# Reordering the step of two cross-attention layers: queries, keys and values, values product, fold, scores, then the whole output; plain keys and values in the first group

## The chip, the cores and the metric

The program runs on one core of one Trainium2 chip. The core has five engines that run side by side, each working through its own list of instructions in order: TensorE (PE in the profile; PEld is its weight load), VectorE (DVE), ScalarE (ACT), GpSimd (POOL) and SyncE (SP), whose list here only starts DMA transfers. The metric is the time of one execution on the device in microseconds (us); the number given for a kernel is the median of the runs shown.

## The reference, cut to what matters

Thirty-two sequences of 64 rows (2048 rows in all, width 512) go through two layers, each a cross-attention and a feed-forward part with residuals.

```python
x = x + xattn0(layernorm(x), ctx, ctx, mask1, wq, wk, wv, wo)   # 32 query heads, 8 key/value heads of 128
x = x + ffn0(layernorm(x), 4-bit weights, scales, zeros)        # silu(gate) * up, width 1376
x = x + xattn1(layernorm(x), ctx, mask0, ...)                   # same sizes; q and k rms-normed over the head
x = x + memory(layernorm(x), ...)                               # top-8 of 128 slots, gated
# xattn0:  q = rope(h @ wq);  k = rope(ctx @ wk);  v = ctx @ wv
#          w = softmax(where(mask, q @ k.T / sqrt(128), -1e9));  out = (w @ v) @ wo
```

`ctx` (32 x 64 x 512) is the same in both layers. Everything is float32.

## The kernel before, in words

**Steps.** Rows are handled in four chunks of 512 (`NCH` = 4, a chunk being eight sequences), heads in eight groups `g` of four query heads and one key/value head (`NKV` = 8). An attention layer is a loop of 32 steps `(g, c)` over groups and, inside, chunks (`Attention.run`, from L753). TensorE does, per step, six kinds of work; the names are those of the PSUM tiles in the profile:

- P: the queries of the next step, normed rows times `wq` (`project_q` L503, through `quarters` L222)
- KV: keys and values of the next step, context times `wkv` (`project_kv` L397)
- po: the values product of this step, probabilities times values (`values` L672)
- pm: layer 1 only, a fold of sums of squares for the rms norms (`norms` L546)
- S: the scores of the next step (`scores` L575)
- O: this step's output, `oT` times `wo`, added to the rows `x` (`out_product` L698, `join` L265)

**Seven products.** P, O and KV use a Strassen-like scheme: operands are cut 2 x 2 and seven block products take the place of eight. `PRODUCTS` (L181) names the left and right block of each product. Blocks 0 to 3 are the operand (two of them, blocks 1 and 2, are later overwritten), blocks 4 to 6 are sums, made on POOL by `left_sums` (L183) or `right_sums` (L194), four operations per operand. Products 1, 2 and 4 of O need none of the left sums; products 6, 5, 3 and 7 do. The products share PSUM tiles: 6 is added onto 1's tile after that has been copied out or added, 3 onto 5's, 7 onto 6's. There are six PSUM tiles `mm` for all of P, KV, po, pm and O, and one double tile `st` for S.

**The way from P and KV to S.** In layer 0, `quarters` copies each quarter of the queries out of PSUM on ACT (`h`, L237), adds on DVE (L514), makes a turned copy on ACT (`rq`, L494), multiplies by cosine and sine on DVE (L497, L498) and adds into `qT` on POOL (L499). The keys go the same way from `kx` through `rk` to `kT`. There are two tiles `tmp` for the turned copies. S needs all of `qT` and `kT`. In layer 1, instead of the rotation, squares are made and summed; pm folds the sums, `qs` is made on DVE and POOL raises it to the power -1/2 (`qr`, L277).

**The rest of a step.** `softmax` (L592) is a generator whose pieces run on DVE, ACT and POOL between the products of an output. `turn_v` (L474) transposes the values on DVE and writes them through 16 DMAs into the one tile `v`. The four po tiles are copied to `oT` on ACT (L693).

**The order in the text of a step.** For step `i` the kernel before writes: the last five products of the output of step `i-1` (`output_rest` L716: 4, 6, 5, 3, 7) with the softmax of step `i` between them; P of `i+1`; po of `i`; KV of `i+1`, with the copies of po and the first half of `left_sums(oT)` written into it (L431 to L434); the second half of `left_sums(oT)`; the first two products of the output of step `i` (`output_first` L708: 1, 2), in layer 1 with pm between; S of `i+1`.

**What sets the real order.** The lists of the engines are made when the program is built. The framework plays the program through with its own estimates of durations, and on each engine takes, of the instructions whose inputs and buffers are ready, the one that is written first. So an instruction written later can come ahead when an earlier one isn't ready in the estimate. `tc.issue_after(ins)` only adds that what is inside comes behind `ins` in its engine's list. On the chip the lists are fixed.

**Context and weights.** A chunk's context is two tiles `ctx` (two buffers, so one chunk at a time), loaded on SP after KV of the step before has read them (`load_ctx` L106). The first time a chunk is met, its four raw blocks are loaded, `ctx_sums` (L121) makes the sums on POOL (eight operations) and stores all seven blocks in `kept`; later loads take the seven blocks from there. In the kernel before that is group 0 of layer 0. `wq` and `wo` share two buffers, `wkv` has one. `att0.start` (L744) does KV and P of the first step.

**Buffers the change touches.** `half` (4) holds `kx`, `vx`, `vt` and the quarters `h`; `m2` (4) holds normed rows, spread columns of the softmax and the raw mask, chunk by chunk (`load_mask` L153, `mask_flags` L158); `sp` (1) holds the softmax's `s`.

Of the kernel before, what the change touches and what calls it, by code (L numbers as in the profile page):

```python
# [44 lines left out]
def tile_xattn_ffn_2_layers(ctx: ExitStack, tc: tile.TileContext, a: dict, out: bass.AP):  # L45
# [105 lines left out]
    mraw = {}  # L151

    def load_mask(c):  # L153
        w = NH * KH * S
        mraw[c] = m2_tile(f"mraw{c}")
        nc.sync.dma_start(mraw[c][:, 0:w], a["mask1"][:, c * w : (c + 1) * w])

    def mask_flags(c):  # L158
        w = NH * KH * S
        nc.vector.tensor_scalar(  # L160
            minv[:, c].rearrange("p f q -> p (f q)"), mraw[c][:, 0:w], 0.0, None, ALU.is_equal
        )
# [189 lines left out]
    class Attention:  # L352
# [44 lines left out]
        def project_kv(self, g, c, ctxT, copies=lambda js: None, sums=lambda: None):  # L397
# [4 lines left out]
            kx, vx = half_tile(f"kx{n}"), half_tile(f"vx{n}")  # L402

            def mul(which, ps=None):
                new = ps is None
                if new:
                    ps = mm_tile(f"KV{which}_{n}")
                l, r = PRODUCTS[which]
                for k in range(2):
                    nc.tensor.matmul(  # L410
                        ps[:, lo],
                        wkv[:, l, k, :],
                        ctxT[k][:, r, :],
                        start=(new and k == 0),
                        stop=(k == 1),
                        skip_group_check=True,
                    )
                return ps

            def copy(dst, cols, ps):  # L420
                return nc.scalar.copy(dst[:, cols], ps[:, lo]).ins
# [4 lines left out]
            copies((0, 1, 2))  # L426
            x = mul(1)
            with tc.issue_after(copy(kx, lo, x)):
                copies((3,))
            sums()  # L430
            y = mul(2)  # L431
            w = mul(5)
            copy(vx, hi, w)
            add(kx, lo, y)  # L434
            mul(6, x)
            copy(kx, hi, x)
            mul(3, w)
            add(kx, hi, w)
            k, rest = self.finish_k(n, kx)
            mul(7, x)  # L440
            copy(vx, lo, x)
            add(vx, hi, x)
            self.keyed = rest()
            add(vx, lo, mul(4))
# [29 lines left out]
        def turn_v(self, g, c, vx):  # L474

            n = f"{self.L}_{g}_{c}"
            vt = half_tile(f"vt{n}")
# [194 lines left out]
        def values(self, g, c, v, probs):  # L672
# [18 lines left out]
            def copies(js):  # L691
                for j in js:
                    ins = nc.scalar.copy(o5[:, j], po[j].rearrange("p (x q) -> p x q", q=S))  # L693
                self.copied = ins.ins

            return oT, copies
# [11 lines left out]
        def output_first(self, g, c, oT, middle=lambda: None):  # L708
# [3 lines left out]
            middle()  # L712
            self.out_add(c, 0, 0, self.out_product(g, c, oT, 2))
            return g, c, oT, x

        def output_rest(self, g, c, oT, x, pieces=None, middle=lambda: None):  # L716

            at = (0, 1, 2, 4) if self.L == 0 else (0, 2, 2, 4)  # L720
            result = []

            def behind(k):
                if pieces is not None:
                    for _ in range(at.count(k)):
                        result[:] = [next(pieces)]

            behind(0)
            z = self.out_product(g, c, oT, 4)
            behind(1)  # L730
            self.out_add(c, 1, 0, z)
            self.out_product(g, c, oT, 6, x)
            self.out_add(c, 0, 1, x)
            behind(2)
            middle()
            self.out_add(c, None, 1, self.out_product(g, c, oT, 5), 1)
            behind(3)
            self.out_add(c, 0, 1, self.out_product(g, c, oT, 3))
            behind(4)
            self.out_product(g, c, oT, 7, x)  # L740
            self.out_add(c, 1, None, x, 2)
            return result[0] if result else None

        def start(self):  # L744
            left_sums(self.wkv[0], HD)
            ctx_sums(0, self.ctx)
# [6 lines left out]
        def run(self, hooks, joined, after, between=lambda c: None, tail=lambda: None, late={},  # L753
# [8 lines left out]

            def ctx_of(i):
                return load_ctx(steps[i][1], f"{self.L}_{steps[i][0]}_{steps[i][1]}")

# [6 lines left out]
            for i, (g, c) in enumerate(steps):  # L772
                more = i + 1 < len(steps)
                if c == NCH - 1 and g + 1 < NKV:
                    self.load_kv(g + 1)
# [807 lines left out]
```

## Time and profile before

| | us |
|---|---|
| median of 3 runs | 2889.42 |
| lowest and highest | 2886.56, 2892.95 |
| the profiled execution | 2894.53 |
| its span, first to last instruction | 2892.7 |
| layer 0's attention, from the third values product to the 31st | 158.09 to 1185.24 |
| layer 1's attention, from the second to the 30th | 1743.45 to 2692.06 |

The span is 1.8 us shorter than the profiled execution's time; what lies around it is not in the profile. Busy shares are averages over stages. The digits of the profile's second part are tenths of a slice of 72.3 us. A timeline row has start, duration, engine, line, operation, tiles and count; in square brackets is the idle time of the engine before it and what ended that. TensorE's matmuls are pipelined and their ends modelled, so the distance between the starts of two groups is a better measure of a group's length than its own duration, which overlaps the next.

### The profile page before, as it was taken

What the parts mean: (1) busy time and instruction counts of PE and PEld (TensorE: products, weight loads), DVE (VectorE), ACT (ScalarE), POOL (GpSimd) and SP (SyncE); (2) the same over time, 40 slices, a digit from 0 to 9 for tenths busy, and PEclk for the clock granted to TensorE, in tenths of its full rate; (3) what the DMA queues carried; (4) which work ended last, traced back from release to release, by engine and by line L of the source; (5) the groups of instructions that cost most, each with busy time, mean ns of one, the idle gap of its engine ahead of it and who ended that gap; (6) DMA issues with size and microseconds to landing.
All of it is one profiled execution on the core that took longest, in us unless ns stands there. A gap on an engine that the chain in (4) does not pass through costs nothing.

```text
span 2892.7 us, 42394 instructions
## 1 busy us (share of the span) xinstructions
PE 2783.6 (96%) x15974; PEld 2272.0 (79%) x15974; DVE 2031.9 (70%) x3109; ACT 886.4 (31%) x1609; POOL 1391.9 (48%) x1147
## 2 busy tenths in 40 slices
PE   5999999999999999999999989999999999999998
PEld 4787777777877787788888778888888888888775
DVE  6778888877787777855665666666666666666667
ACT  2433333333333333321111232222222222222244
POOL 6654545454545454553333445454545454545332
PEclk8999999999999999999999999999999999999999
DMA  5232222222222222200000112222222222222111
GB/s 188 64 106 73 81 74 80 70 75 73 85 66 81 65 81 73 63 28 23 23 22 9 62 59 81 74 81 74 81 73 81 73 89 85 88 74 82 45 33 59
DMA packets 238098, 202.21 MB, mean 70 GB/s; under 512 B 157333, under 2 KB 213773, under 8 KB 237895
## 3 DMA queue, kind: packets, MB, share of 16 engines
q1 hardware_dynamic: 237319, 198.46, 21.7%
q8 instruction: 127, 2.08, 0.3%
q10 hardware_dynamic: 576, 1.05, 0.1%
q14 instruction: 76, 0.62, 0.1%
HBM read 171.11 MB, written 11.53 MB: 63 GB/s over the span
## 4 chain that ended last, share of the span: by engine, by line
PE 65%; DVE 15%; ACT 8%; POOL 5%; issue 5%; SPq 1%; DMA 1%; DVEq 0%; ACTq 0%; POOLq 0%
PE P L212 25%; PE O L212 18%; PE KV L410 9%; PE D L212 4%; PE S L583 4%; ACT rq L494 3%; PE po L684 2%; DVE x L272 2%; ACT oT L693 2%; POOL qT L499 1%; DVE rq L498 1%; DVE h L514 1%; SPq L483 1%; DVE h L497 1%; ACT rk L494 1%
## 5 line engine op out<-in xcount | busy, mean ns | idle before, releaser
L212 PE MATMUL O<-wo,oT 128*128 128x256 f32 x3584 | 820.0, 384 | 0.7 <-DVE x L272 0.5
L212 PE MATMUL P<-xnT,wq 128*128 128x256 f32 x3584 | 791.0, 380 | 10.1 <-ACT h L237 9.8
L212 PEld LDWEIGHTS O<-wo,oT 128*128 128x128 f32 x3584 | 672.6, 190 | 126.7 <-issue 23.9
L212 PEld LDWEIGHTS P<-xnT,wq 128*128 128x128 f32 x3584 | 680.8, 190 | 110.4 <-ACT h L237 15.6
L410 PE MATMUL KV<-ctx,wkv 128*128 128x256 f32 x1736 | 414.5, 390 | 30.8 <-ACT oT L693 23.2
L410 PEld LDWEIGHTS KV<-ctx,wkv 128*128 128x128 f32 x1736 | 321.6, 191 | 119.9 <-ACT oT L693 34.1
L664 POOL TENSOR_TENSOR s<-s,ib 128x512 f32<-128x512 f32 x128 | 168.6, 1339 | 475.5 <-DVE ib L343 465.6
L272 DVE TENSOR_TENSOR x<-x,O 128x512 f32<-128x512 f32 (+1 forms) x448 | 365.5, 816 | 44.5 <-PE O L212 44.2
L237 ACT COPY h<-P 128x512 f32<-128x512 f32 (+1 forms) x352 | 202.4, 575 | 633.9 <-PE P L212 609.9
L658 ACT ACTIVATE s<-s 128x1024 f32<-128x1024 f32 x64 | 67.7, 1057 | 803.4 <-DVE s L656 803.4
L499 POOL TENSOR_TENSOR qT<-h,rq 128x512 f32<-128x512 f32 x128 | 163.2, 1275 | 228.1 <-DVE rq L498 177.0
L212 PE MATMUL P<-xnT,wgu 128*128 128x256 f32 (+1 forms) x1232 | 271.4, 380 | 0.2
L212 PEld LDWEIGHTS P<-xnT,wgu 128*128 128x128 f32 (+1 forms) x1232 | 229.7, 187 | 40.2 <-DVE x L272 4.1
L497 DVE TENSOR_TENSOR h<-h,cosT 128x512 f32<-128x512 f32 x128 | 146.5, 1145 | 91.8 <-ACT rq L494 91.5
L187 POOL TENSOR_TENSOR oT<-oT 128x512 f32<-128x512 f32 x64 | 81.4, 1272 | 251.3 <-ACT oT L693 251.3
L494 ACT COPY rq<-h 64x512 f32<-64x512 f32 x256 | 157.9, 617 | 142.4 <-DVE h L514 115.3
L424 DVE TENSOR_TENSOR kx<-kx,KV 128x256 f32<-128x256 f32 x128 | 53.3, 417 | 171.8 <-PE KV L410 158.4
L1063 DVE TENSOR_TENSOR h<-h,P 128x512 f32<-128x512 f32 (+1 forms) x96 | 61.1, 640 | 128.6 <-PE P L212 92.9
L1070 POOL TENSOR_TENSOR hT<-h,h 128x512 f32<-128x512 f32 (+1 forms) x48 | 56.6, 1182 | 192.6 <-DVE h L1063 192.6
L693 ACT COPY oT<-po 128x512 f32<-128x512 f32 x256 | 139.9, 602 | 24.4 <-PE po L684 23.7
L583 PE MATMUL S<-qT,kT 128*32 128x256 f32 x2048 | 125.5, 386 | 16.6 <-POOL qT L499 9.5
L684 PE MATMUL po<-s,v 32*128 32x256 f32 x2048 | 131.8, 391 | 9.1 <-POOL s L664 8.4
(270 smaller groups left out, 3483.9 us busy)
## 6 DMA issues: line engine op xcount, KB each, us to landing
ctx<-kept SPq DMA_DIRECT2D x118, 896.0 KB
v<-vt SPq DMA_DIRECT2D x1024, 16.0 KB
wq<-in_L_wq SPq DMA_DIRECT2D x32, 256.0 KB
wo<-in_L_wo SPq DMA_DIRECT2D x32, 256.0 KB
wq<-in_L_wqT SPq DMA_DIRECT2D x32, 256.0 KB
wo<-in_L_woT SPq DMA_DIRECT2D x32, 256.0 KB
kept<-ctx SPq DMA_DIRECT2D x6, 896.0 KB
wgu<-in_qweight_gu SPq DMA_DIRECT2D x40, 128.0 KB
```

The source lines that it names most:

```text
L187: tt(b[4], b[2], b[3], ALU.add)
L212: ins = nc.tensor.matmul(pv[0:w, m, :], left[:, l, k, m * P : m * P + w], right[:, r, k, :], start=(first and m == 0 and k == 0), stop=(k ...
L237: last_copy = nc.scalar.copy(t[size], ps[size]).ins
L272: return nc.vector.tensor_tensor(dst, dst, src, ALU.add).ins
L410: nc.tensor.matmul(ps[:, lo], wkv[:, l, k, :], ctxT[k][:, r, :], start=(new and k == 0), stop=(k == 1), skip_group_check=True,)
L494: nc.scalar.copy(t[lo:hi], x[HD - hi : HD - lo])
L497: nc.vector.tensor_tensor(view(x), view(x), over(cosT), ALU.mult)
L499: return nc.gpsimd.tensor_tensor(dst(None), dst(x), dst(t), ALU.add).ins
L583: nc.tensor.matmul(s5[j * KB : (j + 1) * KB, f, e], kT[:, f, e, j], qT[:, f * 4 + j].rearrange("p h q -> p (h q)"), start=True, stop=True,)
L664: nc.gpsimd.tensor_tensor(sv[:, f], sv[:, f], ib[:, f * W : (f + 1) * W].unsqueeze(1).to_broadcast([P, KH, W]), ALU.mult,)
L684: nc.tensor.matmul(po[j][:, f * W : (f + 1) * W], v[rows, f, e], probs[rows, f, e], start=(e == 0), stop=(e == KH - 1),)
L693: ins = nc.scalar.copy(o5[:, j], po[j].rearrange("p (x q) -> p x q", q=S))
```

## The change

The diff does four things.

1. **Order of a step.** For step `i` the text is now: P of `i+1`, KV of `i+1` (in the very first step KV before P), po of `i`, the copies to `oT`, the values' transpose, pm, S of `i+1`, `left_sums(oT)`, and then all seven products of the output of step `i` (`output`: 1, 2, 4, 6, 5, 3, 7) with the softmax of step `i+1` between them. `output_first` and `output_rest` are gone, the sums of `oT` are written in one piece, and the copies of po are no longer written into KV. S keeps an `issue_after(last_matmul)`, which now is the last matmul of P.
2. **Plain keys and values in group 0 of layer 0.** There, eight block products take the place of seven, on the raw blocks (32 matmul records of 128x256 in place of 28); K is finished first and copied in one piece, then V. No sums of `wkv` or of the context are made for them.
3. **Sums of the context one group later.** `ctx_sums` runs in the steps before group 1's KV, so groups 0 and 1 load raw blocks, and `kept` is used from group 2 on.
4. **Buffers and loads.** `vx` and `vt` move from `half` to `m2`; the mask is loaded and turned into flags whole, in the `sp` tile, in place of by chunk; loads and sums of the next group's `wkv` and `wq` move from the last chunk's step to the one before it.

```diff
+    def load_mask():
+        mraw.append(sp_tile("mraw"))
+        nc.sync.dma_start(mraw[0].rearrange("p f w -> p (f w)"), a["mask1"])
+
+    def mask_flags():
...
@@ -394,54 +396,65 @@
-        def project_kv(self, g, c, ctxT, copies=lambda js: None, sums=lambda: None):
+        def project_kv(self, g, c, ctxT):
...
-            kx, vx = half_tile(f"kx{n}"), half_tile(f"vx{n}")
-
-            def mul(which, ps=None):
+            kx, vx = half_tile(f"kx{n}"), m2_tile(f"vx{n}")
+
+            def mul(l, r, ps, cols, first, last):
+                for k in range(2):
...
+            if self.L == 0 and g == 0:
+                for i, x in ((0, kx), (1, vx)):
+                    ps = mm_tile(f"pkv{i}_{n}")
+                    for f, cols in enumerate((lo, hi)):
+                        mul(2 * i, f, ps, cols, f == 0, False)
+                        mul(2 * i + 1, 2 + f, ps, cols, False, True)
+                    nc.scalar.copy(x, ps)
+                    if i == 0:
+                        k, rest = self.finish_k(n, kx)
+                rest()
+                return k, vx
+
+            def product_of(which, ps=None):
...
-            copies((0, 1, 2))
-            x = mul(1)
-            with tc.issue_after(copy(kx, lo, x)):
-                copies((3,))
-            sums()
-            y = mul(2)
-            w = mul(5)
+            x = product_of(1)
+            copy(kx, lo, x)
+            y = product_of(2)
+            w = product_of(5)
             copy(vx, hi, w)
             add(kx, lo, y)
-            mul(6, x)
+            product_of(6, x)
             copy(kx, hi, x)
-            mul(3, w)
+            product_of(3, w)
             add(kx, hi, w)
             k, rest = self.finish_k(n, kx)
-            mul(7, x)
+            product_of(7, x)
             copy(vx, lo, x)
+            rest()
             add(vx, hi, x)
-            self.keyed = rest()
-            add(vx, lo, mul(4))
+            add(vx, lo, product_of(4))
             return k, vx
...
         def turn_v(self, g, c, vx):
 
             n = f"{self.L}_{g}_{c}"
-            vt = half_tile(f"vt{n}")
+            vt = m2_tile(f"vt{n}")
...
-        def output_first(self, g, c, oT, middle=lambda: None):
+        def output(self, g, c, oT, pieces=None, halfway=lambda: None, ended=lambda: None):
+
+
+            def piece():
+                return next(pieces) if pieces is not None else None
 
             x = self.out_product(g, c, oT, 1)
             self.out_add(c, 0, 0, x)
-            middle()
             self.out_add(c, 0, 0, self.out_product(g, c, oT, 2))
-            return g, c, oT, x
-
-        def output_rest(self, g, c, oT, x, pieces=None, middle=lambda: None):
-
-
-
-            at = (0, 1, 2, 4) if self.L == 0 else (0, 2, 2, 4)
-            result = []
-
-            def behind(k):
-                if pieces is not None:
-                    for _ in range(at.count(k)):
-                        result[:] = [next(pieces)]
-
-            behind(0)
-            z = self.out_product(g, c, oT, 4)
-            behind(1)
-            self.out_add(c, 1, 0, z)
+            piece()
+            self.out_add(c, 1, 0, self.out_product(g, c, oT, 4))
             self.out_product(g, c, oT, 6, x)
             self.out_add(c, 0, 1, x)
-            behind(2)
-            middle()
+            piece()
+            halfway()
             self.out_add(c, None, 1, self.out_product(g, c, oT, 5), 1)
-            behind(3)
+            piece()
             self.out_add(c, 0, 1, self.out_product(g, c, oT, 3))
-            behind(4)
             self.out_product(g, c, oT, 7, x)
             self.out_add(c, 1, None, x, 2)
-            return result[0] if result else None
+            ended()
+            return piece()
 
         def start(self):
-            left_sums(self.wkv[0], HD)
-            ctx_sums(0, self.ctx)
+            if self.L == 1:
+                left_sums(self.wkv[0], HD)
             left_sums(self.wq[0], engine=nc.vector if self.L == 0 else nc.gpsimd)
             k, vx = self.project_kv(0, 0, self.ctx)
             self.ctx = load_ctx(1, f"{self.L}_0_1")
@@ -759,102 +757,94 @@
...
             scales = self.norms(0, 0, kpart, part)
-            st = self.scores(0, 0, kT, qT)
+            *_, probs = self.softmax(0, 0, self.scores(0, 0, kT, qT), scales)
...
                 if more:
-                    if c == NCH - 1:
-                        left_sums(self.wkv[g + 1], HD)
-                    if self.L == 0:
-                        ctx_sums(steps[i + 1][1], ctxT)
+                    if self.L == 0 and following[0] == 1:
+                        ctx_sums(following[1], ctxT)
                     if c == 0:
                         right_sums(self.wo[g])
-                    qT, part = self.project_q(*steps[i + 1])
-                    if c == NCH - 2 and g + 1 < NKV:
-                        self.load_q(g + 1)
-                    if i + 2 == len(steps):
-                        ahead[0]()
+                    if i == 0:
+                        (kT, kpart), vx = keys()
+                        qT, part = queries()
+                    else:
+                        qT, part = queries()
+                        if i + 2 == len(steps):
+                            ahead[0]()
+                        if done and self.L == 1:
+                            after(before[1])
+                        (kT, kpart), vx = keys()
                 else:
                     tail()
-                if done and self.L == 1 and more:
+                oT = self.values(g, c, v, probs)
+                pieces = None
+                if more:
+                    v = self.turn_v(*following, vx)
+                    scales = self.norms(*following, kpart, part)
+                    with tc.issue_after(last_matmul):
+                        st = self.scores(*following, kT, qT)
+                    pieces = self.softmax(*following, st, scales)
+                self.pooled = left_sums(oT)
-                oT, copies = self.values(g, c, v, probs)
...
-                if more:
-                    (kT, kpart), vx = self.project_kv(
-                        *steps[i + 1], ctxT, copies, lambda: left_sums(oT, parts=(0,))
-                    )
-                    if i + 2 < len(steps):
-                        ctxT = ctx_of(i + 2)
-                    v = self.turn_v(*steps[i + 1], vx)
-                    if self.L == 0:
-                        with tc.issue_after(self.keyed):
-                            self.pooled = left_sums(oT, parts=(1,))
-                    else:
-                        self.pooled = left_sums(oT, parts=(1,))
-                elif self.L == 0:
-                    self.pooled = left_sums(oT)
-                if done and self.L == 0 and more:
+                elif done and self.L == 0:
                     with tc.issue_after(self.pooled):
...
-                before = self.output_first(g, c, oT, middle)
-                if more:
-                    with tc.issue_after(last_matmul):
-                        st = self.scores(*steps[i + 1], kT, qT)
...
+                    if c == NCH - 2 and g + 1 < NKV:
+                        with tc.issue_after(self.pooled):
+                            left_sums(self.wq[g + 1])
+
+                def ended():
+                    if c == NCH - 2 and g + 1 < NKV:
+                        left_sums(self.wkv[g + 1], HD)
+
+                probs = self.output(g, c, oT, pieces, halfway, ended)
+            joined(steps[-1][1])
...
-    load_mask(0)
+    load_mask()
...
```

## The prediction, made before the changed kernel ran

> **What bounds the kernel now.** First the page's busy times and slices.
>
> ```profile
> PE 2783.6 (96%) x15974; PEld 2272.0 (79%) x15974; DVE 2031.9 (70%) x3109; ACT 886.4 (31%) x1609; POOL 1391.9 (48%) x1147
> ...
> PE   5999999999999999999999989999999999999998
> ```
>
> TensorE is the bound; only the first slice of 72.3 us is half empty. Next the busy times by stage: the start, layer 0's attention, layer 1's.
>
> ```profile
> 0.00:107.69 107.69, 70.99 (x369) 57.03 (x370) 72.77 (x123) 31.91 (x55) 70.31 (x90) 0.89 0.42 139
> 158.09:1185.24 1027.15, 990.59 (x5730) 807.48 (x5729) 816.49 (x1105) 363.47 (x648) 515.13 (x398) 1.00 0.24 76
> 1743.45:2692.06 948.61, 948.59 (x5941) 782.56 (x5940) 626.01 (x972) 263.65 (x487) 466.09 (x327) 1.00 0.26 80
> ```
>
> After window, length and PE busy come the other engines, clock and DMA. The start leaves 107.69 - 70.99 = 36.7 us idle. Layer 1's 27 steps take 35.13 us each with no idle time. Layer 0's 28 steps take 36.68 on the mean, 1.3 of it idle by the records. A layer 0 step on PE, from the timeline:
>
> ```profile
> 698.05 12.25 PE L212 MATMUL P<-xnT,wq 128*128 128x256 f32 x56
> 710.23 2.01 PE L684 MATMUL po<-s,v 32*128 32x256 f32 x32
> 712.17 7.09 PE L410 MATMUL KV<-ctx,wkv 128*128 128x256 f32 x28
> 719.10 3.62 PE L212 MATMUL O<-wo,oT 128*128 128x256 f32 x16
> 722.99 1.93 PE L583 MATMUL S<-qT,kT 128*32 128x256 f32 x32 [0.28 <-POOL kT L499]
> 724.85 8.90 PE L212 MATMUL O<-wo,oT 128*128 128x256 f32 x40
> ```
>
> O runs 8.74 / 40 = 0.218 us per record by starts. I take 0.2157 as the bare pace (P: 12.08 of its 12.18). From P's end to S are 722.99 - 710.23 = 12.76 us; the work in between is po 1.94 + KV 28 x 0.2157 = 6.04 + O 16 x 0.2157 = 3.45, together 11.43. So 1.33 us is lost between P and S, in an undisturbed step of 35.53. What fixes S is the way of the keys, on three engines:
>
> ```profile
> 713.64 1.56 ACT L693 COPY oT<-po 128x512 f32<-128x512 f32 x3
> ...
> 717.64 0.42 DVE L424 TENSOR_TENSOR kx<-kx,KV 128x256 f32<-128x256 f32 x1 [1.26 <-PE KV L410]
> 718.15 1.24 ACT L494 COPY rk<-kx 64x512 f32<-64x512 f32 x2 [1.07 <-DVE kx L424]
> 719.42 1.16 DVE L497 TENSOR_TENSOR kx<-kx,cosT 128x512 f32<-128x512 f32 x1 [1.37 <-ACT rk L494]
> ...
> 721.66 1.27 POOL L499 TENSOR_TENSOR kT<-kx,rk 128x512 f32<-128x512 f32 x1 [1.63 <-DVE rk L498]
> ```
>
> From the end of the last `kx` add (718.06) to S are 4.93 us, now covered by KV's last two products and O's first two (16 records, 3.45).
>
> **Part 1, layer 0's new order.** KV comes straight after P and no longer waits for the copies of po. It gains a conflict instead: its sixth product reuses the tile of the first, whose copy may stand behind ACT's last `rq` copies, which end 3.39 after P's end (713.62). Product 6 would start at 3 x 0.863 = 2.6, and starts at 3.39 + 0.4 = 3.8 at worst: a wait of 0 to 1.25. The `kx` add follows product 3 and, in DVE's list, the last query rotation, which ends 5.8 after P (716.05): it ends between 4.9 and 6.3. S comes 4.93 later, at 9.85 to 11.2. PE's own work until then is KV 6.04 + po 1.94 = 7.98. So 1.9 to 3.2 us of PE are uncovered, where 1.33 were: O, the old cover, is now written behind S, and also can't start until four copies of po (1.56 + 0.63) are done, at about 10.3. I take 3.2, since `rq` copies, rotations and `kx` adds stand in these lists now. What is late elsewhere (the 36.68 - 35.53 = 1.15 us mean, from steps where POOL sums `wo` or DVE does constants) moves S in either order alike.
>
> What can fill the gap is the next step's P: its rows and `wq` are there, two PSUM tiles are free, and the builder takes what is ready. This trace never shows P taken ahead on PE; POOL shows it (at 30.43 the sums of `wo`, written for the first step of the loop, stand before `kT` of the start). The builder fills only the gap that it sees. Bounds: nothing filled, 3.2 - 1.33 = +1.9 per step; nearly all, leaving 0.6, -0.7. I take 1.7 filled (eight records, one product), leaving 1.5: +0.2. Over the 27 steps outside the start: +5 us, between -19 and +51.
>
> At this gap a rule of the clock matters. The trace: P's 24 records after a wait of 3.37 us (39.19) took 7.13, where 24 x 0.2175 = 5.2 would be the pace; KV after a wait of 1.66 (346.46) kept its pace. So a 3.2 us gap lies just inside. The Trainium skill, "TensorE: Matmul & The Clock Gate", section on why this matters for your kernels, warns of idle gaps over about 3 us between bursts, since the clock then falls to half. By that rule an unfilled gap in every step would cost some 1.9 us more, 27 x 1.9 = 51, and the second rival below would end near 2970 instead of 2919; I stay with the row of 1.66 and 3.37 as ends.
>
> **Part 2, the start.** Its waits on PE:
>
> ```profile
> 23.33 1.22 PE L410 MATMUL KV<-ctx1first,wkv 128*128 128x256 f32 x2 [4.91 <-POOL ctx1first L197]
> 39.19 7.13 PE L212 MATMUL P<-xnT,wq 128*128 128x256 f32 x24 [3.37 <-ACT h L237]
> 55.80 3.64 PE L583 MATMUL S<-qT,kT 128*32 128x256 f32 x32 [9.48 <-POOL qT L499]
> ```
>
> Plain KV needs no sums: from 16.1, 14 records at the 0.43 that the first ones show and 18 at 0.216, to 26.0 instead of 28.7. P then runs 12.2 instead of 17.6 (its wait was for a `half` tile, and `vx`, `vt` leave that pool): to 38.2. Queries rotated in the steady 7.23: S at 45.5, 10.3 earlier. KV of the second step (8.71) goes into that wait, but the gap of part 1 opens behind po: -8.7 + 3.2. Step 1 (37.31) comes to about 36.3. Sum -17; between -8 (the first two waits alone) and -28 (chunk 1's rows also ready sooner; P starts 10.2 after S now). Plain KV costs 4 x 0.216 = 0.86 in two more steps: +2. The whole mask is 512 KB ahead of `x` and `wo` on SP's queue; `wo` is used only after 91, so I cost it at nothing; without that cover it is under 3 us, by the 139 GB/s row.
>
> **Part 3, context sums in group 1.** Eight POOL operations of 0.73 (53.13 to 57.89) in each of four steps, beside TensorE; two stores on SP's queue between `v` and the next load. POOL's queue then delays `qT`: step 4, which has `wo` sums, took 38.74 against 35.54, so 0 to 3.2 per step. I take 1.0: +4.
>
> **Part 4, layer 1.** Now P 12.18, po 1.94, KV 6.15, O 1.82, pm 0.26, O 1.92, S 1.86, O 9.00. In the new order P and KV join, O is one piece: 12.18 + 6.05 + 1.94 + 0.26 + 1.86 + 12.2 and 0.2 for `oT`'s copies, which end 0.2 after S: 34.7, so -0.46. Keys are ready: `kT` takes 1.47 on DVE. But `qr` (POOL, 3.54) now stands before the sums of `oT`: pm ends 8.3 after P, `qr` at 12.5, block 5 at 15.1; product 6 wants it at 15.6. With two mask additions (2.5) in between it waits 2.0. Bounds -0.46 and +1.5; I take -0.35, 28 steps: -10. Moved loads of `wq` and `wkv` keep 20 us and more ahead of their use; nothing.
>
> **Sum.** -17 + 2 + 4 + 5 - 10 = -16, against the profiled 2894.5 (span 2892.7 and 1.8 around it): 2878.5. That execution is 5.1 above the median, so 2873.
>
> **Rivals.** First, the gap is filled entirely: -19 for +5, 2849. For it: P is always ready; against: the builder's durations lie below the real ones, or S wouldn't wait 0.28 now. Second, the slower one: nothing is filled, +51 for +5, at +30 or 2919. Its place is PE between po and S in layer 0; it decides from a loss of 1.33 + 21 / 27 = 2.1 us per step on. For it: 4.93 us of key work with 1.94 of po as cover; against: the free PSUM tiles. Third, layer 1's product 6 waits for POOL, +0.9 a step (between -0.35 and +1.5): +25 for -10, 2908. For it: `qr`'s 3.54; against: 0.5 of slack. That the order on PE doesn't change is excluded only for layer 1, where nothing is late; in layer 0 it is the first rival in another form.
>
> **How the numbers follow.** The forecast 0.38 (its own range 2858 to 2888), filled 0.18, unfilled 0.32, `qr` 0.12. A difference under 0.2% (5.8 us) can't be told from none in this kernel. Faster: 0.18 and 0.32 of the forecast, 0.50; within: 0.07; slower: the rest, 0.43. The range reaches to both outer cases with 5 to 10 us for the start: 2842 to 2930.
>
> **What would show it.** P records between po and S or O, and S starting 10 to 11.5 us after P's end with a wait on `kT` of about 1.5; 3 if rival two holds. First S near 45. Layer 1 steps of 34.7 to 34.9; a wait of O on `oT` L188 for the third. The forecast is wrong if S's wait is long in every step, if KV waits on `kx` or `vx` copies by more than 1.3, or if the start stays near 107.

## The result, and the profile after

The changed kernel takes 2996.87 us (median; 2996.01 to 2999.56) beside 2889.01 for the kernel before on the same chip: a ratio of 1.0374, 95% interval 1.0356 to 1.0392. It is slower by 108 us; the forecast was 2873, between 2842 and 2930. The profiled span went from 2892.7 to 2994.2, +101.5. All accounts by place below are in that span.

First the lines that answer those shown of the kernel before. The page of the changed kernel, busy times and slices:

```profile
PE 2773.4 (93%) x15990; PEld 2302.5 (77%) x15990; DVE 2001.6 (67%) x3090; ACT 887.0 (30%) x1601; POOL 1368.3 (46%) x1143
...
PE   6888899999999999899999989999999999999997
```

TensorE is busy no longer than before (2773.4 us against 2783.6), so the 101.5 us are time in which it waits. The busy times by stage, cut at the same events as before (start; from po of step 2 to po of step 30; from po of step 33 to po of step 60, which are the second and the 29th of layer 1, not the 30th; steps counted from 0 through both layers; after window and length come PE, PEld, DVE, ACT and POOL, then clock, DMA share and GB/s):

```profile
0.00:107.76 107.76, 70.72 (x377) 57.37 (x378) 70.57 (x114) 30.92 (x50) 48.95 (x61) 0.89 0.33 106
168.24:1243.90 1075.66, 983.64 (x5729) 816.21 (x5728) 805.66 (x1100) 365.43 (x646) 533.93 (x431) 0.99 0.24 77
1804.27:2796.52 992.25, 945.93 (x5941) 801.14 (x5940) 605.37 (x973) 260.74 (x486) 452.05 (x327) 0.98 0.25 77
```

Layer 1, which had no idle time before (948.59 busy in 948.61), now has 46 us of it. To see where, measure each step from the start of its po to the start of the next:

| stretch | before | changed | both sums behind `oT`'s | last kernel of this study |
|---|---|---|---|---|
| start to po of step 2 | 158.09 | 168.24 | 168.88 | 152.39 |
| steps 2 to 5 | 146.72 | 172.41 | 147.33 | 145.50 |
| steps 6 to 30 | 926.35 | 942.36 | 931.97 | 916.02 |
| steps 31 and 32, with the feed-forward part | 512.29 | 521.26 | 520.35 | 515.85 |
| steps 33 to 59 | 948.61 | 992.25 | 935.59 | 935.83 |
| the rest | 200.64 | 197.68 | 199.78 | 196.71 |
| span | 2892.7 | 2994.2 | 2903.9 | 2862.3 |

In layer 1, 20 of the 27 steps take 34.36 us where they took 35.13, a gain of 15.4. The other seven, each the step of chunk 2 of a group, take 43.17 to 43.80, a loss of 59. One of them, from the timeline of the changed kernel:

```profile
1838.64 2.01 PE L697 MATMUL po<-s,v 32*128 32x256 f32 x32
1838.74 1.23 SPq L382 DMA_DIRECT2D wkv<-in_L_wkT  x1
...
1840.02 0.50 SPq L382 DMA_DIRECT2D wkv<-in_L_wvT  x1
...
1842.59 5.45 PE L214 MATMUL O<-wo,oT 128*128 128x256 f32 x24
...
1846.02 0.73 POOL L189 TENSOR_TENSOR wkv<-wkv 128x256 f32<-128x256 f32 x1 [16.84 <-DMA wkv<-in_L_wvT]
...
1848.87 3.55 POOL L279 TENSOR_TENSOR qr<-qs,nhalf 128x20 f32<-128x20 f32 x1
1852.38 1.27 POOL L189 TENSOR_TENSOR oT<-oT 128x512 f32<-128x512 f32 x1
...
1853.72 1.27 POOL L190 TENSOR_TENSOR oT<-oT 128x512 f32<-128x512 f32 x1
...
1855.04 9.25 PE L214 MATMUL O<-wo,oT 128*128 128x256 f32 x32 [7.01 <-POOL oT L190]
```

Read it from the bottom. O's product 6 needs block 5 of `oT`, the result of L190 on POOL. That operation stands in POOL's list behind `qr`, and `qr` behind the four sums of the next group's `wkv`; and the first of those waits for a transfer that SP started at 1840.02 and that lands at 1846.02. The copies to `oT` had been done by 1842.7, `qs` by 1841.2. So POOL stood idle with work at hand because the head of its list was not ready. The wait on PE is 7.01; the 32 matmuls behind it then take 9.25 where 32 x 0.2157 = 6.90 is their pace, 2.35 more. Together 9.36: the step's 43.72 less 34.36.

The waits of the changed kernel by name (total, times, longest):

```profile
POOL wkv L189 <- DMA wkv<-in_L_wvT: 98.0, 6, 17.0
...
PE O L214 <- POOL oT L190: 74.5, 17, 7.3
...
PE S L596 <- POOL kT L512: 48.4, 30, 2.1
...
PE xta L318 <- DVE xna L304: 27.3, 10, 12.0
...
POOL wkv L189 <- DMA wkv<-in_L_wv: 19.6, 6, 4.6
```

In the kernel before, PE's longest lists of waits were KV on the copies to `oT` (23.2) and the transposes of the start on the scaled rows (15.6); O on `oT` was not among them. (Some 12 us of the waits for rows, in both, are those of the very first transposes.) The wait of S on `kT` is the gap in layer 0. Here it is in a chunk 2 step of that layer, which also shows the wait of O on `oT`:

```profile
788.20 2.01 PE L697 MATMUL po<-s,v 32*128 32x256 f32 x32
...
790.53 1.27 POOL L512 TENSOR_TENSOR kT<-kx,rk 128x512 f32<-128x512 f32 x1 [1.73 <-DVE rk L511]
...
791.85 1.93 PE L596 MATMUL S<-qT,kT 128*32 128x256 f32 x32 [1.64 <-POOL kT L512]
...
793.72 5.45 PE L214 MATMUL O<-wo,oT 128*128 128x256 f32 x24
...
796.39 0.73 POOL L189 TENSOR_TENSOR wkv<-wkv 128x256 f32<-128x256 f32 x1 [4.59 <-DMA wkv<-in_L_wv]
...
800.61 1.26 POOL L190 TENSOR_TENSOR oT<-oT 128x512 f32<-128x512 f32 x1
...
801.92 4.37 PE L214 MATMUL O<-wo,oT 128*128 128x256 f32 x19 [2.76 <-POOL oT L190]
```

There is no P between po and S: nothing fills the gap. An ordinary step of layer 0 takes 36.44 to 36.51.

In steps 2 to 5 the sums of the second group's context stand ahead of `oT`'s on POOL too; in step 2 the changed kernel has eight of them and four of `wkv`:

```profile
172.55 0.73 POOL L199 TENSOR_TENSOR ctx<-ctx 128x256 f32<-128x256 f32 x1 [1.45 <-DMA ctx<-in_ctxT]
...
176.29 0.72 POOL L189 TENSOR_TENSOR wkv<-wkv 128x256 f32<-128x256 f32 x1
...
183.33 1.26 POOL L190 TENSOR_TENSOR oT<-oT 128x512 f32<-128x512 f32 x1
...
184.65 9.89 PE L214 MATMUL O<-wo,oT 128*128 128x256 f32 x32 [6.19 <-POOL oT L190]
```

Last the start of the changed kernel. S comes at 42.40 instead of 55.80, as meant, and then PE finds nothing:

```profile
42.40 3.64 PE L596 MATMUL S<-qT,kT 128*32 128x256 f32 x32 [7.44 <-POOL qT L512]
...
53.74 0.71 DVE L345 STREAM_TRANSPOSE ib<-m1s 128x512 f32<-128x512 f32 x1
...
54.37 3.77 DVE L304 TENSOR_SCALAR xna<-x,mva,rsa 128x512 f32<-128x512 f32 x4
...
55.03 1.09 PE L318 MATMUL xta<-ident,xna 128*128 128x128 f32 x4 [8.99 <-DVE xna L304]
```

The scaling of chunk 1's rows (DVE, 54.37) is listed behind the whole first softmax, whose last DVE operation is the spread of the sums at 53.74; KV of the second step is listed behind the transposes. po of step 0 starts at 79.11 (before: 78.78), po of step 2 10.2 later than before.

So there were three suspects: POOL's list (the sums of `wkv`, and of the context), the uncovered keys in layer 0, and DVE's list at the start. The runs below take them one by one.

### The profile page after: what moved, and what is told of

The parts are those of the page before. It is cut to its first block, busy times and chain, and to the rows that moved or that the text cites. A ratio compares the mean times of both kernels' runs of the same rounds, so it can differ in the third digit from the quotient of the medians.

```text
span 2994.2 us, 42269 instructions
## 1 busy us (share of the span) xinstructions
PE 2773.4 (93%) x15990; PEld 2302.5 (77%) x15990; DVE 2001.6 (67%) x3090; ACT 887.0 (30%) x1601; POOL 1368.3 (46%) x1143
## 4 chain that ended last, share of the span: by engine, by line
PE 69%; DVE 12%; POOL 7%; ACT 5%; DMA 4%; issue 3%; SPq 1%; DVEq 0%; ACTq 0%; POOLq 0%
PE P L214 29%; PE O L214 21%; PE KV L408 7%; PE D L214 4%; PE S L596 3%; ACT rq L507 3%; DVE h L510 2%; PE po L697 2%; DMA wkv<-in_L_wvT 2%; DVE rq L511 1%; DVE h L527 1%; DMA wkv<-in_L_wv 1%; DVE x L274 1%; POOL qr L279 1%; ACT rk L507 1%
## 5 line engine op out<-in xcount | busy, mean ns | idle before, releaser
L214 PEld LDWEIGHTS O<-wo,oT 128*128 128x128 f32 x3584 | 692.5, 195 | 206.5 <-POOL oT L190 81.3
L408 PE MATMUL KV<-ctx,wkv 128*128 128x256 f32 x1652 | 376.0, 381 | 15.7 <-ACT vx L437 11.7
L408 PEld LDWEIGHTS KV<-ctx,wkv 128*128 128x128 f32 x1652 | 310.7, 190 | 71.2 <-ACT vx L437 22.9
L677 POOL TENSOR_TENSOR s<-s,ib 128x512 f32<-128x512 f32 x128 | 161.4, 1282 | 384.2 <-DVE ib L345 319.7
L279 POOL TENSOR_TENSOR qr<-qs,nhalf 128x20 f32<-128x20 f32 x32 | 113.4, 3543 | 300.0 <-DVE qs L584 300.0
L510 DVE TENSOR_TENSOR h<-h,cosT 128x512 f32<-128x512 f32 x128 | 139.8, 1092 | 112.2 <-ACT rq L507 112.2
L705 ACT COPY oT<-po 128x512 f32<-128x512 f32 x256 | 131.4, 600 | 95.1 <-PE po L697 95.1
L596 PEld LDWEIGHTS S<-qT,kT 128*32 128x32 f32 x2048 | 65.7, 112 | 105.0 <-POOL kT L512 60.4
```

The source lines that it names most:

```text
L214: ins = nc.tensor.matmul(pv[0:w, m, :], left[:, l, k, m * P : m * P + w], right[:, r, k, :], start=(first and m == 0 and k == 0), stop=(k ...
L279: return nc.gpsimd.tensor_tensor(dst, src, nhalf[:, : src.shape[-1]], ALU.pow).ins
L408: nc.tensor.matmul(ps[:, cols], wkv[:, l, k, :], ctxT[k][:, r, :], start=(first and k == 0), stop=(last and k == 1), skip_group_check=True,)
L510: nc.vector.tensor_tensor(view(x), view(x), over(cosT), ALU.mult)
L596: nc.tensor.matmul(s5[j * KB : (j + 1) * KB, f, e], kT[:, f, e, j], qT[:, f * 4 + j].rearrange("p h q -> p (h q)"), start=True, stop=True,)
L677: nc.gpsimd.tensor_tensor(sv[:, f], sv[:, f], ib[:, f * W : (f + 1) * W].unsqueeze(1).to_broadcast([P, KH, W]), ALU.mult,)
```

## The experiments

**One order edge for the sums of `wkv`.** All work stays; the sums come behind `oT`'s on POOL.

```diff
                 def ended():
                     if c == NCH - 2 and g + 1 < NKV:
-                        left_sums(self.wkv[g + 1], HD)
+                        with tc.issue_after(self.pooled):
+                            left_sums(self.wkv[g + 1], HD)
```

> The changed kernel (2996.9), with one edit: the sums of the next group's wkv must be listed on POOL behind the sums of oT (an order edge, no other work changed). Theory, POOL's list: in chunk 2 of each group the sums of oT stand behind sums that wait for a transfer; with the edge layer 1's seven long steps (43.2 to 43.8) fall to 34.4 to 35, -63 together, and layer 0's third steps (38.1 to 39.5) to about 36.5, -11, with some 3 more in step 2: about 2920 (2910 to 2930), and no wait of O on oT over 1 us outside group 1. Rival, the transfer: the load of wkv at its new place is itself too late or holds up what SP carries behind it; then KV or po takes over the wait, the seven steps stay above 41, and the time above 2980.

Measured: 2929.7 us, 1.0120 of before (1.0104 to 1.0136), 67 below the changed kernel. (The kernel before stood at 2889.0 beside the changed kernel, and at 2893.7, 2893.2 and 2889.3 beside the experiments; a difference of two medians from different groups is good to some 5 us.) Layer 1's seven steps fall from 43.2 to 43.8 to 35.47, layer 0's third steps, from step 6 on, to 36.5 to 36.7; O waits for `oT` four times only, 14.9 in all, and those are in steps 2 to 5. The transfer at its new place holds up nothing that PE needs: the rival is out. Of the forecast gain of 77, 67 came; most of what is missing (7 x 1.1) is that the seven steps stop at 35.47 and not 34.4.

**The same for the context's sums.**

```diff
-                        ctx_sums(following[1], ctxT)
+                        with tc.issue_after(self.pooled):
+                            ctx_sums(following[1], ctxT)
```

> The changed kernel (2996.9), with one edit: the context's sums of the second group are listed on POOL behind the sums of oT of the step before. Theory, POOL's list: the waits of O on oT in steps 3 to 5 (3.7 us in the one looked at) go, steps 3 to 5 fall from 42.98, 42.55 and 41.95 to about 38.5 to 39, step 2 by less since wkv's sums still stand ahead there: -8 to -16, 2981 to 2989. Rival: the sums are needed by KV of the same step, so KV waits for them instead, and the time stays within 4 us of 2997.

Measured: 2980.19, 1.0299 (1.0277 to 1.0321), 17 below the changed kernel. Steps 3, 4 and 5 fall from 42.98, 42.55 and 41.95 to 37.85, 36.43 and 36.44; KV does not take the wait over.

**Both edges.**

> Both edits together. Theory, POOL's list: the two add, -77 and -12, to 2902 to 2915, with step 2 also under 39; what is left against the kernel before (2889) is the start and the gap ahead of S in layer 0 (0.9 a step, 25 steps), less 0.77 in each of layer 1's ordinary steps. Rival, that the new order is slower in itself: above 2950 even then.

Measured: 2905.57, 1.0039 (1.0024 to 1.0054), 91 below the changed kernel. Step 2, where each edge alone left the other's sums in front (42.90 and 40.48), is now 36.62. A chunk 2 step of layer 1, to set beside the one above:

```profile
1805.52 3.54 POOL L279 TENSOR_TENSOR qr<-qs,nhalf 128x20 f32<-128x20 f32 x1 [12.10 <-DVE qs L584]
...
1806.85 11.49 PE L214 MATMUL O<-wo,oT 128*128 128x256 f32 x52
...
1810.38 1.27 POOL L190 TENSOR_TENSOR oT<-oT 128x512 f32<-128x512 f32 x1
...
1817.74 0.72 POOL L189 TENSOR_TENSOR wkv<-wkv 128x256 f32<-128x256 f32 x1
```

O runs through without a wait, and POOL comes to `wkv` at 1817.74, when the transfer is long done. The edges add and take away no work, and PE's list has the same order as before them; so 90 of the 101.5 us of span were the place of these sums in POOL's list. The table's third column shows what is left: +10.8 at the start, +0.6 and +5.6 in layer 0, +8.1 around the feed-forward part, -13.0 in layer 1.

**The transfer or the sums?** The changed kernel as it was, without the loads of `wkv` behind the first group.

```diff
         def load_kv(self, g):
+            if g > 0:
+                self.wkv[g] = self.wkv[0]
+                return
             kv = wkv_tile(f"wkv{self.L}_{g}")
```

> The changed kernel (2996.9) without the loads of wkv for the groups after the first: every group of a layer reads the first group's tile and the sums run on it again, at the same place of POOL's list (the outputs are then those of other weights; nothing else is left out). Theory, the wait for the transfer inside POOL's list: the sums of wkv (2.8 us) still stand ahead of qr and the sums of oT but can start as soon as the last KV product has read the tile, 7 us earlier; layer 1's seven long steps fall from 43.2 to 43.8 to 34.4 to 35.5, layer 0's third steps to about 36.5: 2915 to 2930. Rival, the work of the sums ahead of oT's is what costs: 2.8 us on POOL stay, the long steps stay above 37 and the time above 2945.

Measured: 2943.78, 1.0176 (1.0160 to 1.0192), between the two theories. In layer 1 the list has the sums of `wkv` ahead of `qr` and `oT`'s as before, and the seven steps take 34.9: there the wait for the transfer is the whole loss, and 2.8 us of sums in front cost only 0.5. In layer 0 the steps of chunk 2 from step 6 on got no better (39.3 to 40.8), for another reason: with no transfer to wait for, the builder put the sums still earlier, ahead of `kT`.

```profile
490.62 1.20 POOL L193 TENSOR_TENSOR wkv<-wkv 128x256 f32<-128x256 f32 x1
491.78 1.17 POOL L192 TENSOR_TENSOR wkv<-wkv 128x256 f32<-128x256 f32 x1
492.92 1.26 POOL L515 TENSOR_TENSOR kT<-kx,rk 128x512 f32<-128x512 f32 x1
...
494.23 3.64 PE L599 MATMUL S<-qT,kT 128*32 128x256 f32 x32 [3.01 <-POOL kT L515]
```

S now waits 3.01 us and runs at half pace after that (3.64 where the same 32 matmuls took 1.93). So in layer 0 the place of the sums costs something even with no transfer.

**The move alone, in the old order.** The kernel before, with the load of `wkv` right behind chunk 2's KV and its sums behind that step's last output product.

```diff
-                if c == NCH - 1 and g + 1 < NKV:
-                    self.load_kv(g + 1)
...
+                    if c == NCH - 2 and g + 1 < NKV:
+                        self.load_kv(g + 1)
                     if i + 2 < len(steps):
                         ctxT = ctx_of(i + 2)
...
+                    if c == NCH - 1 and g + 1 < NKV:
+                        left_sums(self.wkv[g + 1], HD)
-                    if c == NCH - 1:
-                        left_sums(self.wkv[g + 1], HD)
```

> The kernel before (2889 to 2894) with the move of wkv alone: its load right behind KV of chunk 2's step, its sums behind the last output product of that step. Theory, it is the place in the list and not the move: in the old order oT's sums are written between KV's products and the builder lists them ahead of wkv's; nothing that PE needs soon stands behind the wait, and the time stays within 0.3% of before. Rival, the move itself is the loss: seven steps of layer 1 longer by 5 to 9, +35 to +65.

Measured: 2894.35, 1.0002 (0.9992 to 1.0011): no difference. In layer 1 POOL's list has `oT`'s sums and `qr` first and the sums of `wkv` behind them, and by then the transfer has landed or nearly so:

```profile
POOL wkv L187 <- DMA wkv<-in_L_wvT: 1.2, 4, 0.5
```

That is 1.2 us in all, where it was 98.0. The same move that costs 67 us in the new order costs nothing in the old one. Layer 1's chunk 2 steps do get 1.0 to 1.5 longer (36.1 to 36.6), with waits of O for additions to the rows on DVE (8.4 in all); steps 2 to 32 give as much back.

**S behind O's first two products again, in layer 0.** Both edges, and this for the cover of the keys.

```diff
             self.out_add(c, 0, 0, self.out_product(g, c, oT, 2))
+            if made is not None:          # layer 0: scores and softmax of the next step
+                pieces = made()
             piece()
```

> Both edits, and in layer 0 S is written behind O's first two products again, as in the kernel before; keys and values stay ahead of po. Theory A, the gap is S's order (S waits 1.64 us for kT with only po as cover): the wait on kT goes, -1.2 to -1.6 in 27 steps, -32 to -44 against both_behind. Theory B, the cover that is gone is KV between po and O: O's first product then waits for the copies of po, which end about 2.4 us after po does (ACT 2.05 from 0.02 after po's end, and the pipe), so PE waits 2.4 where it waited 1.64: +0.75 in 27 steps, +20 against both_behind.

Measured: 2919.16, 1.0087 (1.0070 to 1.0105), 13.6 above the kernel with both edges; theory A is out. PE's waits of this kernel:

```profile
PE O L214 <- ACT oT L705: 34.5, 29, 2.5
```

The 46.5 us in which S waited for `kT` (29 times) are gone, and O waits 34.5 us for the copies of po in their place, 1.2 each time and not the 2.4 of theory B. P and KV wait more for copies on ACT (14.3 for 7.5, and 15.5 for 12.3), and so the waits of the two kernels are about equal: in steps 6 to 30 they sum to 58.2 us here and 60.1 with both edges alone. That these 25 steps are 7.5 us longer all the same lies inside the matmuls: by the distances between starts, less the waits, O's take 314.4 us for 308.1 and P's 306.1 for 303.0. Whether they run slower or stand in stalls too short to be listed is not shown. With KV ahead of po there is one gap behind po, whichever product stands there; in the kernel before, KV stood there and waited 23.2 us for the same copies.

**A product of P in the gap.** Both edges, and in 21 of layer 0's steps the first query product of the step after next is written ahead of S.

```diff
                     scales = self.norms(*following, kpart, part)
+                    if self.L == 0 and 3 <= i < len(steps) - 2 and c != NCH - 2:
+                        g2, c2 = steps[i + 2]
+                        self.early[g2, c2] = mm_tile(f"P1_0_{g2}_{c2}")
+                        product(1, self.early[g2, c2], self.wq[g2], xnT[c2])
                     with tc.issue_after(last_matmul):
```

> Both edits (2905.6), and in layer 0 the first query product of the step after next (8 matmuls, 1.73 us) is written between po and S, in the 21 steps from the fourth on where its weights are there (not in chunk 2). Theory, PE only lacks work in the gap and nothing but the list keeps it from having some: S waits 0 to 0.3 us for kT instead of 1.64, those steps fall from 36.45 to about 34.9, -33: 2868 to 2878. Rival: the product holds a PSUM tile through the whole of O, O's products wait for the adds on DVE to free tiles, and the gain is given back: above 2895.

Measured: 2887.11, 0.9979 (0.9969 to 0.9988), 18.5 below the kernel with both edges. The steps fall from 36.45 to 35.56, not to 34.9:

```profile
828.07 1.99 PE L214 MATMUL P<-xnT,wq 128*128 128x256 f32 x8 [0.57 <-DVE vx L441]
...
829.99 1.93 PE L597 MATMUL S<-qT,kT 128*32 128x256 f32 x32
...
831.86 10.41 PE L214 MATMUL O<-wo,oT 128*128 128x256 f32 x47
```

S and O wait for nothing, so the rival (a tile held through O) is out; but the product itself waits 0.57 for a PSUM tile that `vx`'s addition sets free, and ends later than `kT`. Some 0.9 of the 1.6 is to be had.

**Chunk 1's rows ahead of the first softmax.** Both edges, and layer 0's first hook is called before the softmax of step 0.

```diff
-            *_, probs = self.softmax(0, 0, self.scores(0, 0, kT, qT), scales)
+            st0 = self.scores(0, 0, kT, qT)
+            for hook in hooks.get((0, 0), ()):
+                hook()
+            *_, probs = self.softmax(0, 0, st0, scales)
```

> Both edits (2905.6), and the statistics and scaling of chunk 1's rows are written ahead of the first step's softmax, as they stood in the kernel before. Theory, at the start DVE's list is the limit (the scaling of chunk 1's rows stands behind the whole first softmax, and the transposes wait 9 us for it at 55): po of step 2 starts 6 to 10 us earlier than at 168.9, and the time is 2896 to 2900. Rival: the first softmax, later by the same DVE work, moves po of step 0 back by as much, and the time is within 3 us of 2905.6.

Measured: 2893.45, 1.0002 (0.9992 to 1.0011), 12 below the kernel with both edges. po of step 0 starts at 65.36 instead of 79.73, po of step 2 at 157.74 instead of 168.88. The transposes fall into the wait for `qT` (before S of step 0), while S of step 1, behind po of step 0, still waits for `qT`:

```profile
41.91 1.11 PE L318 MATMUL xta<-ident,xna 128*128 128x128 f32 x4 [4.74 <-DVE xna L304]
42.82 2.55 PE L408 MATMUL pkv<-ctx,wkv 128*128 128x256 f32 x6
...
45.60 1.93 PE L596 MATMUL S<-qT,kT 128*32 128x256 f32 x32 [0.22 <-POOL qT L512]
...
72.61 3.46 PE L596 MATMUL S<-qT,kT 128*32 128x256 f32 x32 [5.25 <-POOL qT L512]
```

**The four edits together.**

> The four edits together: both sums behind oT's, chunk 1's rows ahead of the first softmax, and the early query product. Theory, they mend different places and add: 2905.6 - 12.1 (rows) - 18.5 (early product) = 2875, between 2868 and 2882, faster than the kernel before by 0.6%. Rival, the losses share a place (an earlier start meets rows or loads that are not there yet): 2884 or more, not to be told from before.

Measured: 2878.41, 0.9954 (0.9938 to 0.9971). They add, within 4 us.

**The other rows too.** As the last one, with the rows of chunks 2 and 3 in layer 0 and of the last chunk in layer 1 written one step earlier.

```diff
+                if more:
+                    for hook in hooks.get(following, ()):
+                        hook()
                 oT = self.values(g, c, v, probs)
```

> As the kernel with the four edits, and in both layers the rows that a step's hook makes ready (chunks 2 and 3 in layer 0, the last chunk in layer 1) are written one step earlier, behind keys and values instead of behind the next softmax. Theory, what is left at the start of both layers is again DVE's list (transposes wait for the scaling of rows: 22 us in layer 0, 6.4 us in step 32): steps 0 and 1 fall from 48.3 and 44.1 to about 40, step 32 from 47 to about 40, -15 to -20: 2855 to 2862. Rival: DVE is full there and the same work ahead of the softmax moves po back, so the steps only trade places: within 5 us of the kernel with four edits.

Measured: 2864.14, 0.9905 (0.9889 to 0.9921): faster than the kernel before by 0.95%. Step 1 falls to 35.62 (forecast 40) and step 32 to 38.90; step 0 only to 45.48, in which S now waits 3.02 for `kT`. The rival is right in part: po of step 0 moves back from 66.43 to 71.30, and step 31 takes 476.95 where it took 473.64. (Of the 22 us of waits for rows that the expectation names, 12 are those of the very first transposes, which every kernel here has.)

## Why the prediction was wrong

**"Moved loads of `wq` and `wkv` keep 20 us and more ahead of their use; nothing."** This is the step that failed, and it carried most of the loss. As to KV it is true. But it looked at the last user alone. The first user is the sums on POOL; they wait at the head of a list, and what stands behind them there (`qr`, the sums of `oT`) is wanted by the output of the very same step. The working named, for a wait, what is queued behind it in the rivals but not here. Measured: 67 us of 108 by one order edge. That the builder listed the sums first because its estimates had the transfer land sooner fits the lists; no run shows those estimates.

**Context sums, "0 to 3.2 per step. I take 1.0: +4".** The edge for them alone took 17 us off, and steps 2 to 5 were 25.7 longer with `wkv`'s in front as well. The price was looked for at `qT`, as with the sums of `wo` in the step taken as a row; the wait was at O, again by the place in the list: eight operations ahead of `oT`'s sums.

**The third rival** had the place right, O's product 6 waiting for POOL, and the wrong cause and price: `qr` alone never delayed it. With `wkv`'s sums out of the way, `qr` runs from 1805.52, L190 ends at 1811.6, and O needs no wait. +0.9 per step was forecast for it, 0 was measured; and the 8.4 by which the seven steps exceed 35.13 came from what stood in front of `qr`.

**Layer 0's gap.** P's end to S was to be 10 to 11.5 us; from KV's start at 781.51 to S at 791.85 are 10.34. The uncovered part was bounded by 1.9 and 3.2, and is 10.34 - 7.98 = 2.36 where 1.33 were. The filling failed: 1.7 filled was taken, none was; that is rival two at a milder size, +0.9 in an ordinary step. In sum, steps 6 to 30 with both edges are only 5.6 longer, close to the forecast +5, but by another way: the ordinary step is longer (36.45 for 35.53), while the mean over all 25 goes from 37.05 to 37.28, since the old order lost time in more of the steps that have other work beside them. That PE only lacked work there is shown by the early product; why the builder took none is not: six PSUM tiles with four of them po's, and 0.57 of wait for one even when the order was written out, speak for tiles and against "two PSUM tiles are free".

**The start, -17.** No run shows this gain. S came at 42.40, even earlier than the 45.5 of the working, but by a slip: 0.43 us is the distance of two records at the start and was taken for that of one, so plain keys and values were put at 9.9 us and took 7.20 (15.51 to 22.71). What was to follow S failed. "KV of the second step (8.71) goes into that wait" and "Step 1 (37.31) comes to about 36.3": the softmax of step 0 is now consumed ahead of the loop, so DVE has it in front of chunk 1's scaling, and steps 0 and 1 took 47.74 and 41.40. With the rows ahead of that softmax, po of step 0 starts 13.4 us earlier than in the kernel before, but steps 0 and 1 still take 48.27 and 44.12 (before: 42.01 and 37.31), and po of step 2 is only 0.35 earlier; in the last kernel it is 5.7 earlier. One part of this is the gap behind po of step 0, where keys and values now stand ahead of P: 3.2 was put for it, and S waits 5.25 for `qT` and then runs at half pace (3.46 for 1.93). What makes up the rest stays open.

**Layer 1, -0.35 a step.** The order itself is better than forecast: 34.36 in the ordinary step, -0.77, outside the bound of -0.46 (the working's own terms give -0.44). The working's own terms sum to 34.49 with no wait; the 0.2 for the copies was not needed, as pm, S and the copies overlap. Keys and values in one run with P, and the output in one piece, are a gain; 13 us of it are left with both edges.

**Not in the working at all:** +9 in steps 31 and 32. Most of it is in step 32 (47.65 for 40.39), where the transposes of the last chunk's rows wait 6.4 us for DVE, the same fault as at the start; the last kernel got that step down to 38.90.

**The range.** With both edges the kernel takes 2905.6, inside the range. Its span is 11.2 over before where -16 was forecast; of these 27 us, 22 are the start and steps 2 to 5 (+11.4 for -11), 8 the steps around the feed-forward part, and layer 1 gives 3 back. The other 91 us of the miss went with the two edges: the wait that was costed at nothing, and the context's sums that were costed at +4. The range had no term for the first, and 3.2 us a step as the most for the second.

## What to carry to other kernels

A moved load is priced at the first instruction that waits for it, and by what stands behind that instruction in its engine's list, not by the distance to the last user. Where lists are made from estimates, work written later that waits for a DMA can land in front of work that is needed now; one order edge is cheap and shows it at once. When a reordering loses, put the old waits and the new waits by name side by side before judging the order: here the order on PE was right in layer 1, and the lists of POOL and DVE that it brought along made most of the loss.

## What the runs showed of the hardware

**Where a wait on TensorE begins to cost twice.** The prediction left the edge between 1.66 and 3.37 us. In the traces of the changed kernel and of the one without loads, waits of 2.42 to 2.76 us ahead of O cost at most 0.11 us in the matmuls of the next 7 us (spacing of starts against that of undisturbed ones, 0.2157 us for O); a wait of 2.95 ahead of P cost 1.8 more, the six of 3.01 ahead of S 1.4 to 2.9, waits of 3.73 to 7.3 ahead of O 1.5 to 3.2. But there is no sharp edge. The same wait of 2.08 us, ahead of the same S, in the kernel with the context's edge alone and in the changed kernel:

```profile
1233.64 3.62 PE L596 MATMUL S<-qT,kT 128*32 128x256 f32 x32 [2.08 <-POOL kT L512]
...
1249.35 1.93 PE L596 MATMUL S<-qT,kT 128*32 128x256 f32 x32 [2.08 <-POOL kT L512]
```

The granted clock was 0.50 behind the first (1234 to 1237) and 1.00 behind the second. So too a wait of 2.76 ahead of O cost 0.1 us in the changed kernel (801.92) and 1.8 in the other (185.47). In all twelve traces, waits from 2.1 to 2.8 us went either way, and none above 2.8 kept the full clock. The Trainium skill, "TensorE: Matmul & The Clock Gate", section on why this matters for your kernels, says to have no idle gaps over about 3 us between bursts; here shorter ones could already bring the lower clock, and the measurement decides. So each of layer 1's waits of 5.9 to 7.3 us cost some 9, and the gap of 1.64 in layer 0 cost only itself.

**DVE beside POOL.** In layer 1's chunk 2 step with both edges, the softmax's subtraction (128x1024) took 2.26 us while POOL ran sums of `wq`, and 1.21 in the step before, where POOL ran none. The Trainium skill, "SBUF — State Buffer", section on the two separate sides, says that a DVE operation with two inputs in SBUF and a GpSimd operation that reads SBUF shut each other out for a whole instruction; these two rows agree. It may be part of why those steps stay 1.1 us above the others: in each of them P waits some 0.63 us for a copy on ACT, and ACT has that copy behind the exponential that follows the subtraction. But in the kernel without loads the subtraction took 2.26 in the same steps too, and there P did not wait and the steps took 34.9; so the cause of the 1.1 us is left open.
